# First batch element: x on ScalarE's queue, matrix pieces first on the two others; the last rows ahead of layer four's weights

## The chip, the cores and the metric

The kernel runs on one core of a Trainium2 chip. The core has five engines that run side by side, each with its own stream of instructions: TensorE (PE), VectorE (DVE), ScalarE (ACT), GpSimd (POOL) and SyncE (SP). They wait for each other through semaphores only. Transfers between device memory and the core's SBUF are issued by an engine into its own DMA queue. Three queues are used here: that of SP, that of ACT and that of POOL. All three feed the same 16 DMA engines. The metric is the device time of one execution in microseconds (us).

## What is computed

x is 16 elements of 1024 nodes by 128 features, adj 16 matrices of 1024 x 1024. All is float32.

```
# first block, per element
degree = adj.sum(-1)
gathered = einsum('bid,bij->bjd', x, adj) / degree
x = layernorm(x + relu(concat(x, gathered) @ W.T + b))
# second block: four layers; layers 3 and 4 also get the outputs of earlier layers as input
src = nodes @ ws + bs;  dst = nodes @ wd + bd;  own = nodes @ wn + bn
upd = concat(rownorm(adj) @ src, own, colnorm(adj).T @ dst)
nodes = tanh(upd @ wu + bu)
x = layernorm(x + nodes_of_layer_4)
```

rownorm and colnorm divide the rows and the columns of adj by their Euclidean norms.

## The kernel before

The elements are worked through one after the other. One matrix of 4 MB stays in SBUF while its element is computed, and the next one is loaded into a second buffer meanwhile. The order of the instructions on every engine is written out by hand: the Python program issues them in the order in which each engine executes them. `hooks` in a layer is a dictionary from the number of a matmul step to a function, which issues work on all engines just before that step.

Only the first element has nothing ahead of it to hide its loads. Its beginning is a program of its own.

- **Loads.** The matrix `a` of element one is cut into eight blocks of 128 rows, `k` of each half `h`. `load_pair(q, i, groups)` loads two blocks (a pair, 1 MB) with one DMA of 256 KB (a piece) for each group of 32 partitions. Groups 0 and 1 are issued by SP, 2 and 3 by POOL, for each of four pairs; the first two pairs are the second half. `load_nodes(q, h)` loads half an x, four DMAs of 64 KB, whose runs are 512 bytes long; the matrix has runs of 4096 bytes. `w0n` is the weight of the first block, 128 KB; `b0r` is its bias, read for all partitions.
- **First block.** TensorE runs three idle matmuls of zeros (`idle`, six passes, since a float32 matmul has two records), then transposes the second half of x (`xtr`, `to_xT(1)`), then `w0n` (`w0tr`). ACT copies both out of PSUM. Then follow the products of x and weights (`px`, four blocks), and for each pair the products `pa` of x and matrix as it arrives. ACT squares the blocks (`square`), DVE sums their rows (`degree`), POOL adds the squares. `pg` are the products of gathered nodes and weights; DVE turns them into x1n, with statistics, and `written` scales them. For block 0 of the second half `written` is an ACT instruction (L541), for the others one of DVE. `x1tr` transposes them.
- **Weights.** Each layer's weights are folded: `fetch_weights` loads ws, wd, wn and wu, `fold_begin` transposes the first three (`wtr`) and multiplies the biases (`bm`), `fold_end` multiplies by wu (`wm`) and saves the result to device memory (`wsave`). PSUM results called `small` share two banks, so a third one waits until ACT has copied out the first.
- **Transposed matrix.** The source side needs the matrix transposed. `load_rows(0, q, ...)` loads quarter q of the rows in another order (eight DMAs of 128 KB), `scale_rows` multiplies them on ACT by the inverse norms of the rows (eight instructions), `transpose_rows` transposes them on DVE. Quarters 2 and 3 make `at[1]`, 0 and 1 make `at[0]`.
- **Layer one** (`plain_layer`) has 34 matmul steps of two passes: 2 with the own weights, 16 with the matrix (half 1, half 0), 8 with `at[1]` and 8 with `at[0]`, from step 26. `last_loads` issues the loads of layer four's weights and of row quarter 1 on SP.

The DMAs of SP wait for one another through eight counters, which ACT's DMAs share: the ninth is issued when the first has landed. POOL has eight of its own.

Of the kernel before, what the change touches and what calls it, by code (L numbers as in the profile page):

```python
# [23 lines left out]
def adj_resnorm_kernel(ctx: ExitStack, tc: tile.TileContext, x, adj, w0, b0, layers, out):  # L24
# [33 lines left out]
    nc = tc.nc  # L58
    B, N, D = x.shape
    NB = N // P  # L60
# [8 lines left out]
    NJ = NB // 2  # L69
# [41 lines left out]
    ident = one.tile([P, HW], F32, tag="e0", name="ident")[:, :P]  # L111

    def own_weights(wm, l, c):

        if l == 3:
            at = dict(zip(PAIRED[l], (0, P))).get(c, 2 * P + SUMS)
            return wx[l][:, at:at + P]
        if l == 2:
            at = MREST + P * PAIRED[l].index(c)
            return wm[:, at:at + P]  # L120
        return wm[:, CHUNKS[l] + 1, :P]

    def message_weights_of(wm, l, c):

        if l in PAIRED:
            at = 2 * P * (1 + PAIRED[l].index(c)) if c in PAIRED[l] else MREST
            return by_parts(wm[:, at:at + 2 * P])
        return wm[:, 1 + c].rearrange("p (a v c) -> p a v c", a=2, v=2)
# [67 lines left out]
    def fetch_weights(raw, l, q, bc, wm=None):  # L196
        ws, bs, wd, bd, wn, bn, wu, bu = layers[l]
        nch = CHUNKS[l]
        size = max(3 * nch * P, KEPT[l] * 2 * P, WIDTH[l])
        flat = raw.take(size) if wm is None else wm[:, WIDTH[l]:]  # L200
        wr = flat[:, :3 * nch * P].rearrange("p (k c v) -> p k c v", k=3, c=nch)
        for k, w in enumerate((ws, wd, wn)):
            q.dma_start(wr[:, k], w.rearrange("(c p) v -> p c v", p=P))
        wur = raw.take(3 * P).rearrange("p (k v) -> p k v", k=3)
        q.dma_start(wur, wu.rearrange("(c p) v -> p c v", p=P))
        if wm is not None:
            wm = as_chunks(wm, l)
        else:
            wm = as_chunks(flat[:, :WIDTH[l]] if l in PAIRED else flat, l)
        return wr, wur, bc, wm, [raw.take(3 * P).rearrange("p (k v) -> p k v", k=3) for _ in range(nch)]  # L210

    def fold_begin(l, fetched, copy=nc.scalar.copy, later=False):

        wr, wur, bc, wm, wTs = fetched
        for c in range(CHUNKS[l]):
            name = f"wtr{l}_{c}"
            pt = small(name, [BPH, P]) if c < 2 else product(name).rearrange("p (k v) -> p k v", v=P)
            for k in range(3):
                nc.tensor.transpose(pt[:, k], wr[:, k, c], ident)
            copy(wTs[c], pt[:, :3])  # L220
        pm = small(f"bm{l}", [HW]) if CHUNKS[l] == 1 else product(f"bm{l}")
        for k in range(2):
            nc.tensor.matmul(pm[:, k * P:(k + 1) * P], bc[:, k:k + 1].to_broadcast([P, P]),
                             wur[:, PART[k]], start=True, stop=True)
        nc.tensor.matmul(pm[:, 2 * P:2 * P + 1], wur[:, PART[2]], bc[:, 2:3], start=True, stop=True)

        def biases():
            if l in PAIRED:
                nc.scalar.copy(by_parts(wm[:, :2 * P]), pm[:, :2 * P].rearrange("p (a v c) -> p a v c", a=2, v=2))
            else:  # L230
                nc.scalar.copy(wm[:, 0], pm[:, :2 * P])
            nc.scalar.activation(bout[l], pm[:, 2 * P:2 * P + 1], AF.Identity, bias=bc[:, 3:4])

        return biases if later else biases()

    def fold_end(l, fetched, chunks=None):
        _, wur, _, wm, wTs = fetched
        for c in range(CHUNKS[l]) if chunks is None else chunks:
            pm = small(f"wm{l}_{c}", [HW]) if c < 2 else product(f"wm{l}_{c}")
            for k in range(3):  # L240
                nc.tensor.matmul(pm[:, k * P:(k + 1) * P], wTs[c][:, k], wur[:, PART[k]],
                                 start=True, stop=True)
            nc.scalar.copy(message_weights_of(wm, l, c), pm[:, :2 * P].rearrange("p (a v c) -> p a v c", a=2, v=2))
            nc.scalar.copy(own_weights(wm, l, c), pm[:, 2 * P:3 * P])
        if l not in PAIRED:
            nc.sync.dma_start(wsave[l], wm.rearrange("p c v -> p (c v)")[:, :WIDTH[l]])
        elif l == 3:
            nc.sync.dma_start(wsave[l], wm)
# [6 lines left out]
    def small(name, shape=(K,)):  # L255
        return ps_s.tile([P, *shape], F32, tag="small", name=name)
# [11 lines left out]
    def product(name, i=None):  # L268
        if i is None:
            return ps_t.tile([P, HW], F32, tag="pt", name=name)  # L270
        return ps_p.tile([P, HW], F32, tag=f"p{i}", name=name)
# [135 lines left out]
    def root_inverses(cols, inv, s):  # L407
        nc.vector.tensor_scalar_max(cols[:, s], cols[:, s], NORM_EPS * NORM_EPS)  # L408
        nc.gpsimd.tensor_tensor(inv[:, s], cols[:, s], mhalf[:, s], ALU.pow)  # L409
# [271 lines left out]
    def load_rows(b, q, st):  # L681


        n = QB // len(st)
        for i, piece in enumerate(st):
            load_rows_piece(b, q, piece, i * n, n)
        return st

    def load_rows_piece(b, q, piece, k, n, groups=range(G)):
        v = adj[b, q * QB * C:(q + 1) * QB * C].rearrange("(k r) (h g j) -> h g r k j", r=C, h=NH, g=G)  # L690
        for g in groups:
            for h in range(NH):
                nc.sync.dma_start(piece[g * C:(g + 1) * C, :, h * P:(h + 1) * P], v[h, g, :, k:k + n])  # L693
        return piece

    def scale_rows(st, q, rinv, which=range(QB)):
        n = QB // len(st)
        for k in which:
            row = st[k // n][:, k % n]
            nc.scalar.activation(row, row, AF.Copy, scale=rinv[:, q * QB + k:q * QB + k + 1])  # L700
# [444 lines left out]
    w0n = one.tile([P, 2 * P], F32, tag="xb", name="w0n")  # L1145
# [4 lines left out]
    def load_pair(q, i, groups):  # L1150
        h, k = PAIRS[i]
        for g in groups:
            q.dma_start(a[g * C:(g + 1) * C, h * BPH + k:h * BPH + k + 2], av[h][g, :, k:k + 2])

    def load_nodes(q, h):
        for g in range(G):
            q.dma_start(xn[g * C:(g + 1) * C, h * BPH:(h + 1) * BPH], xv[h][g])

    idle = one.tile([P, HW], F32, tag="S2", name="idle")
    nc.vector.memset(idle, 0.0)  # L1160
    make_identity(nc, ident)
    load_nodes(nc.sync, 1)
    nc.gpsimd.dma_start(w0n, w0)
    for i in range(4):
        load_pair(nc.sync, i, (0, 1))
        load_pair(nc.gpsimd, i, (2, 3))
        if i == 1:
            load_nodes(nc.gpsimd, 0)
    biases_of = [[b0, *layers[0][1::2], *layers[1][1::2]], layers[2][1::2], layers[3][1::2]]
# [37 lines left out]
    places = {q: Q[i].rearrange("p k (u c) -> p (k u) c", u=2) for q, i in ((2, 2), (3, 3), (0, 4))}  # L1207
    places[1] = one.tile([P, 2 * NJ, HW // 2], F32, tag="T2", name="rows1_0")
    rows, fetched = {}, []
# [8 lines left out]
    def last_loads():  # L1218
        places_left = Places([one.tile([P, NJ, HW], F32, tag="T4", name="raw4").rearrange("p k i -> p (k i)"),
                              one.tile([P, N], F32, tag="x", name="raw4_x"),  # L1220
                              one.tile([P, HW], F32, tag="S4", name="raw4_s")])
        columns.append(places_left.take(len(biases_of[2])))
        fetched.append(fetch_weights(places_left, 3, nc.sync, columns[2]))
        rows[1] = load_rows(0, 1, [places[1]])

    nc.vector.memset(mhalf, -0.5)
    nc.vector.reduce_sum(fold[:, :C], ident.rearrange("p (g c) -> p c g", g=G), axis=AX.X)
# [94 lines left out]
    def written(h, q, write=norm_write):  # L1322
        mv, _, rstd, shift = of_half[h][1]
        v = x1n[:, h * BPH + q]
        write(v, v, (mv, rstd, shift), q)
# [47 lines left out]
    two_stats(1, 2)  # L1373
    root_inverses(cols, inv, slice(NB))
    biases()
    written(1, 0, norm_write_act)
    fold_end(0, fetched[0])
    biases = fold_begin(1, fetched[1], later=True)
    for q in range(1, BPH):
        written(1, q)  # L1380
# [26 lines left out]
    for b in range(B):  # L1407
# [8 lines left out]
        if b == 0:  # L1416
# [23 lines left out]
            def columns0(rows, h, engine=nc.vector):  # L1440
                scale_columns(a, cinv[0], rows, half(h), engine)
# [20 lines left out]
            def fold_last(destination, finish):  # L1462
                bias_columns(2)
                fold_begin(3, fetched[3])

            def first0(destination, finish):
                destination(0, cinv[0])
                columns0(range(NJ), 0)
                scale_rows(rows[1], 1, rinv)
                transpose_rows(rows[1], 1, at)  # L1470
                fold_last(destination, finish)

            def sums0(destination, finish):
                combine_1(y)
# [7 lines left out]
                for i in range(2):  # L1482
# [2 lines left out]
            hooks = {3: lambda *_: inverses(0, st0, NB), 5: weights0, 6: rows0,  # L1485
                     7: lambda *_: scale_rows(rows[0], 0, rinv), 8: cinv0,
                     9: lambda *_: transpose_rows(rows[0], 0, at), 10: second0,
                     14: lambda *_: columns0(range(NJ, NB), 0), 18: first0, 21: lambda *_: fold_end(3, fetched[3]),
                     26: sums0}
            T = {i: one.tile([P, NJ, HW], F32, tag=f"T{i}", name=f"T{i}_0") for i in (2, 3)}  # L1490
            plain_layer(b, 0, feats, t, wm, a, at, f1, "acc", hooks)
# [196 lines left out]
        if nxt:  # L1688
# [4 lines left out]
            rows = {}  # L1693
# [182 lines left out]
```

## Time and profile before

| | us |
|---|---|
| median of 3 runs | 2378.34 |
| lowest and highest | 2377.73, 2379.17 |
| the profiled execution's own time | 2378.45 |
| its span in the trace | 2376.6 |
| TensorE busy in the span | 2364.0 |
| TensorE busy, 0 to 62 us of the span | 55.90 |
| TensorE busy, 62 to 2360 us | 2298.00 |
| TensorE busy, 2360 to 2376.6 us | 10.13 |

The clock granted to TensorE was 0.999 over the span. All times of instructions below are counted from the beginning of the span. In a row of the timeline the first number is the start, the second the time until the group ended, and the brackets hold how long the engine had been idle before it and what released it. In a row of waits the numbers are the total, how often, and the longest. A name such as `wtr<-ident,raw` says what is written and what is read; L and a number is the line. A row of a DMA queue has packets, MB and the time of its packets as a share of 16 engines.

### The profile page before, as it was taken

The numbers are of one execution on the slowest core, as the hardware profiler recorded it, in microseconds if no ns is written. First come the engines' busy times: TensorE is split into PE (matmuls) and PEld (weight loads), VectorE is DVE, ScalarE is ACT, GpSimd is POOL, SyncE is SP. The second block draws the span as 40 slices with busy tenths as digits, with TensorE's granted clock in tenths as the row PEclk, the third lists the DMA queues.
The fourth block names the chain that finished last, engine by engine and source line by source line (L and its number), as shares of the span: only waits on it lengthen the run. The fifth ranks groups of instructions, "written<-read, shape, count | busy, mean of one in ns | idle before, by whom it ended". The sixth has DMA issues, their size and how long they took to land.

```text
span 2376.6 us, 39287 instructions
## 1 busy us (share of the span) xinstructions
PE 2364.0 (99%) x15268; PEld 1148.7 (48%) x15268; DVE 2094.5 (88%) x2830; ACT 980.9 (41%) x1858; POOL 278.5 (12%) x119
## 2 busy tenths in 40 slices
PE   9999999999999999999999999999999999999998
PEld 5455565555655555443534444344443444434444
DVE  7999998998988989889988889898899998998954
ACT  5425335352443524445243452534425334352322
POOL 5000111101111011111011110111100111101100
PEclk9999999999999999999999999999999999999999
DMA  9536263362734527244273442725336263362400
GB/s 226 110 89 144 58 138 76 80 139 49 158 62 98 116 54 166 52 105 106 63 157 70 100 94 72 152 65 121 82 77 145 58 140 75 80 139 49 101 22 22
DMA packets 363909, 232.10 MB, mean 98 GB/s; under 512 B 150758, under 2 KB 334827, under 8 KB 363723
## 3 DMA queue, kind: packets, MB, share of 16 engines
q1 hardware_dynamic: 360698, 226.24, 42.9%
q0 software_dynamic: 1200, 2.50, 0.4%
q8 instruction: 121, 1.98, 0.4%
q10 hardware_dynamic: 1824, 0.85, 0.1%
q14 instruction: 66, 0.53, 0.1%
HBM read 209.66 MB, written 19.84 MB: 97 GB/s over the span
## 4 chain that ended last, share of the span: by engine, by line
PE 97%; DMA 2%; SPq 0%; DVE 0%; ACT 0%; issue 0%; POOLq 0%; POOL 0%; ACTq 0%; DVEq 0%
PE m L1106 45%; PE z L1106 24%; PE pt L261 9%; PE pt_z L261 5%; PE m_f L636 5%; PE m3s L1106 2%; PE z_f L636 2%; PE pw L261 2%; DMA Q<-in_adj_dram 1%; DMA b0r<-in_L_gnn_b_dram 1%; PE pt_p L261 1%; PE z L925 1%; DMA raw<-in_L_gnn_wu_dram 0%; DMA a<-in_adj_dram 0%; DMA rows<-in_adj_dram 0%; SPq L693 0%
## 5 line engine op out<-in xcount | busy, mean ns | idle before, releaser
L1106 PE MATMUL m<-a,t 128*64 128x512 f32 x1008 | 425.1, 593 | 0.0
L1106 PE MATMUL m<-at,t 128*64 128x512 f32 x1008 | 420.4, 592 | 0.0
L1106 PE MATMUL m<-T,S 128*64 128x512 f32 (+1 forms) x1040 | 398.5, 572 | 0.0
L1106 PE MATMUL m<-Q,S 128*64 128x512 f32 x880 | 392.3, 592 | 0.0
L496 POOL TENSOR_TENSOR rs<-ve,mhalf 128x32 f32<-128x32 f32 x30 | 191.6, 6386 | 1019.2 <-DVE ve L494 1019.2
L1106 PE MATMUL z<-at,t 128*64 128x512 f32 (+1 forms) x520 | 229.6, 579 | 0.0
L1106 PE MATMUL z<-a,S 128*64 128x512 f32 x504 | 228.3, 592 | 0.0
L1106 PE MATMUL z<-Q,t 128*64 128x512 f32 (+1 forms) x520 | 227.5, 580 | 0.0
L1106 PE MATMUL z<-a,t 128*64 128x512 f32 (+1 forms) x520 | 227.4, 580 | 0.0
L1106 PE MATMUL z<-at,S 128*64 128x512 f32 x504 | 226.6, 592 | 0.0
L1106 PEld LDWEIGHTS m<-Q,S 128*64 128x64 f32 x880 | 119.4, 137 | 214.9 <-issue 213.2
L1106 PEld LDWEIGHTS m<-T,S 128*64 128x64 f32 x1040 | 128.8, 137 | 141.0 <-issue 135.9
L1106 PEld LDWEIGHTS m<-at,t 128*64 128x64 f32 x1008 | 131.4, 137 | 131.5 <-issue 131.5
L1106 PEld LDWEIGHTS m<-a,t 128*64 128x64 f32 x1008 | 129.7, 137 | 114.0 <-issue 107.0
L958 ACT COPY e<-m 64x512 f32<-64x512 f32 x63 | 36.7, 582 | 340.2 <-PE m L1106 339.8
L1106 PE MATMUL z<-T,t 128*64 128x512 f32 (+2 forms) x400 | 173.0, 575 | 0.0
L409 POOL TENSOR_TENSOR inv<-cols,mhalf 128x16 f32<-128x16 f32 (+1 forms) x16 | 50.0, 3126 | 933.9 <-DVE cols L408 933.9
L448 DVE TENSOR_TENSOR a<-a,cinv 128x512 f32<-128x512 f32 x256 | 155.5, 682 | 0.0
L336 ACT ACTIVATE sq<-a 128x1024 f32<-128x1024 f32 x120 | 125.9, 1050 | 37.5 <-DVE acc L343 23.4
L1106 PEld LDWEIGHTS z<-Q,t 128*64 128x64 f32 x520 | 69.6, 137 | 122.6 <-issue 121.9
L331 ACT ACTIVATE a<-a 128x1024 f32<-128x1024 f32 x120 | 125.4, 1045 | 0.4
L261 PE MATMUL pt<-wm,f1T 128*64 128x128 f32 (+1 forms) x1536 | 120.5, 308 | 0.0
(338 smaller groups left out, 4925.5 us busy)
## 6 DMA issues: line engine op xcount, KB each, us to landing
a<-in_adj_dram SPq DMA_DIRECT2D x120, 512.0 KB, 12.8
rows<-in_adj_dram SPq DMA_DIRECT2D x480, 64.0 KB, 2.2
a<-in_adj_dram SPq DMA_DIRECT2D x240, 128.0 KB, 3.4
wm<-wsave SPq DMA_DIRECT2D x32, 704.0 KB, 4.4
wm<-wsave SPq DMA_DIRECT2D x31, 320.0 KB, 3.0
xs<-in_x_dram SPq DMA_DIRECT2D x60, 128.0 KB, 3.4
cinv<-dr SPq DMA_DIRECT2D x30, 256.0 KB, 6.6
dinv<-dr SPq DMA_DIRECT2D x30, 256.0 KB, 6.6
```

Source lines behind the costliest of these rows:

```text
L261: nc.tensor.matmul(out[s], x[:, s], y, start=start, stop=stop)
L331: nc.scalar.activation(a[:, i, :], a[:, i, :], AF.Copy, accum_out=degree)
L336: nc.scalar.activation(sq, a[:, i, :], AF.Square, accum_out=state["cols"][:, i:i + 1])
L409: nc.gpsimd.tensor_tensor(inv[:, s], cols[:, s], mhalf[:, s], ALU.pow)
L448: engine.tensor_mul(a[:, i, s], a[:, i, s], cinv[:, s])
L496: nc.gpsimd.tensor_tensor(rstd, ve, mhalf[:, :n], ALU.pow)
L636: nc.tensor.matmul(o, x_, y_, start=start, stop=stop)
L925: nc.tensor.matmul(nodes(o) if len(y.shape) == 4 else o, x_, y, start=start, stop=stop)
L958: nc.scalar.copy(e0[high], A[high])
L1106: nc.tensor.matmul(o, x, y_, start=start, stop=stop)
```

## The change

Three things are changed, all of them in the program of element one. The instructions stay the same; only their order on the engines and the queue of four DMAs change.

1. The second half of x is issued by ACT, as its first four instructions, no longer by SP ahead of the matrix. SP begins with its eight matrix pieces. POOL begins with its two pieces of the first pair; the building of the identity matrix (`make_identity`, POOL) and the load of `w0n` follow behind them, ahead of the second pair.
2. `fold_end(0)`, with two ACT copies, is issued ahead of `written(1, 0, norm_write_act)`, with one ACT instruction.
3. In `last_loads` the row quarter 1 is loaded ahead of layer four's weights. Its scaling on ACT is issued at step 11 of layer one, no longer at 18, where it stood ahead of the bias columns and the folding of layer four. These are issued at step 19, and `fold_end(3)` at 22 instead of 21. The transposition of quarter 1 on DVE stays at 18.

```diff
-    make_identity(nc, ident)
-    load_nodes(nc.sync, 1)
-    nc.gpsimd.dma_start(w0n, w0)
+    load_nodes(nc.scalar, 1)
     for i in range(4):
         load_pair(nc.sync, i, (0, 1))
         load_pair(nc.gpsimd, i, (2, 3))
+        if i == 0:
+            make_identity(nc, ident)
+            nc.gpsimd.dma_start(w0n, w0)
         if i == 1:
             load_nodes(nc.gpsimd, 0)
...
+        rows[1] = load_rows(0, 1, [places[1]])
         columns.append(places_left.take(len(biases_of[2])))
         fetched.append(fetch_weights(places_left, 3, nc.sync, columns[2]))
-        rows[1] = load_rows(0, 1, [places[1]])
...
+    fold_end(0, fetched[0])
     written(1, 0, norm_write_act)
-    fold_end(0, fetched[0])
     biases = fold_begin(1, fetched[1], later=True)
...
             def first0(destination, finish):
                 destination(0, cinv[0])
                 columns0(range(NJ), 0)
-                scale_rows(rows[1], 1, rinv)
                 transpose_rows(rows[1], 1, at)
-                fold_last(destination, finish)
...
+                     11: lambda *_: scale_rows(rows[1], 1, rinv),
-                     14: lambda *_: columns0(range(NJ, NB), 0), 18: first0, 21: lambda *_: fold_end(3, fetched[3]),
+                     14: lambda *_: columns0(range(NJ, NB), 0), 18: first0, 19: fold_last,
+                     22: lambda *_: fold_end(3, fetched[3]),
                      26: sums0}
```

## The prediction

> **What bounds the kernel now.** I read the page's busy times first, then who TensorE waited for before and after 62 us, then its timeline in the first 34 us, and last the packets of each DMA queue in short stretches.
>
> ```profile
> PE 2364.0 (99%) x15268; PEld 1148.7 (48%) x15268; DVE 2094.5 (88%) x2830; ACT 980.9 (41%) x1858; POOL 278.5 (12%) x119
> ```
>
> TensorE is busy for 2364.0 of 2376.6 us. Whatever shortens this kernel takes idle time from TensorE, and only 12.6 us are there. Its waits from 0 to 62 us, and then from 62 us to the end:
>
> ```profile
> PE pa L1258 <- DMA a<-in_adj_dram: 1.3, 2, 1.0
> PE wtr L219 <- ACT raw L1185: 1.3, 1, 1.3
> PE bm L223 <- ACT wm L244: 1.3, 1, 1.3
> PE px L1286 <- ACT w0T L1204: 0.7, 1, 0.7
> ...
> PE on L1793 <- DVE f23T L1788: 0.4, 1, 0.4
> ```
>
> The diff can reach three of them: two waits for the matrix (0.33 and 1.01 us), one at `wtr` and one at `bm` (1.28 each). With `px` that is 4.6 us, 0.19%, the most that could be gained. The timeline (start, duration, instruction, idle time before) shows where they sit:
>
> ```profile
> 6.74 0.80 PE L1194 MATMUL xtr<-ident,xn 128*128 128x128 f32 x4
> ...
> 9.97 3.67 PE L1258 MATMUL pa<-a,xn 128*128 128x512 f32 x8 [0.33 <-DMA a<-in_adj_dram]
> 14.65 1.95 PE L1258 MATMUL pa<-a,xn 128*128 128x512 f32 x4 [1.01 <-DMA a<-in_adj_dram]
> ...
> 32.02 0.71 PE L223 MATMUL bm<-raw 128*128 128x128 f32 x4 [1.28 <-ACT wm L244]
> ...
> 32.71 0.63 PE L1330 MATMUL x1tr<-ident,x1n 128*128 128x128 f32 x4
> ```
>
> The first useful work is `xtr`, the transpose of x's second half. It comes before everything else in TensorE's order, and it needs all four x pieces. They were alone on the SP queue and had landed by 4.8 us (issue at 2.1, 2.7 us to landing). The rows that decide are the packets of the queues (packets, MB, share) in 2.5 to 3, 3 to 3.5, 19 to 20 and 22 to 22.5 us, where q1 is SP's and q0 POOL's:
>
> ```profile
> q1 hardware_dynamic: 188, 0.09, 57.6%
> ...
> q0 software_dynamic: 32, 0.11, 75.8%
> q1 hardware_dynamic: 58, 0.02, 17.9%
> ...
> q0 software_dynamic: 66, 0.21, 78.7%
> q1 hardware_dynamic: 67, 0.07, 28.3%
> ...
> q1 hardware_dynamic: 144, 0.07, 44.9%
> ```
>
> Two busy queues move equal numbers of packets, not equal bytes. From 17 to 18 us both carry 4 KB packets: 50 of POOL's to 49, 0.17 MB to 0.16. At 19 us SP carries mostly 512-byte packets (b0 and first weights): still 67 to 66, but 0.07 MB to 0.21. Alone, SP then does 144 such packets in half a microsecond; beside POOL's large ones it did 67 in a whole one. At 3 us x's own packets fell from 188 to 58 per half microsecond, just while w0's 128 KB passed.
>
> **Part 1: x on ACT's queue, matrix first.** x's second half is 512 packets of 512 bytes, 32 per DMA engine, with four completion packets 36. Before, they ran in front of the matrix in SP's queue. Now SP (from 0.74 instead of 2.59 us) and POOL (0.74 instead of 2.21) put 4 KB packets beside them from the start, and each x packet waits for one of each. When x has had its 36 turns, SP has had 36 too, four data and one completion per piece: 7.2 pieces of 256 KB, 1.9 MB. POOL the same, with w0 and small packets among them, some 1.8. With x that is 3.9 MB. By the windows, before had moved 0.55 MB at 5 us and 3.9 at 17.2. The queues fill now at about 2.5 us instead of the lull of 96 to 131 GB/s up to 5 us, worth some 0.4 MB at 0.27 MB/us: 1.5 us. So the last turn comes near 15.7 us, and the slowest DMA engine some 0.5 later (SP's pieces landed while the mean was most of a piece ahead): x lands at 16.2 us. Bounds: 5.5 if queues shared by bytes (256 KB at a third of 0.27 MB/us from 1.8 us, 4.7, and landing), 18.5 if x ended with the whole matrix. I take 16.2, because the 19 us row is the nearest: small packets of a hardware queue beside large ones. At the best rate seen, 0.33 MB/us from 1.8 us on, it is 13.6.
>
> SP can't run dry and free x earlier: SP's and ACT's DMAs share eight completion counters, so SP's pieces 5, 7 and 8 wait for x's pieces 1, 2 and 3, but piece 7 is issued at x's 18th turn while SP holds work to its 30th.
>
> The Trainium skill, "DMA: Bandwidth & Descriptors", section "Queues, rings and completion order", says that each engine round-robins between queue rows by packets; the 67 to 66 agrees. Its section "Issuing engines are not separate DMA queues" says that a second issuing engine only saves issue time; by that rule alone this part would gain at most SP's 1.85 us of issue.
>
> Then TensorE: from `xtr` at 6.74 to `wtr` at 27.69 are 20.95 us, less the waits for the matrix, now long landed, 19.6. `wtr` starts at 16.2 + 19.6 = 35.8, so 8.1 us late. ACT and DVE keep pace: ACT's squares (8 of 1.14 us and two copies) end 14 us after `xtr`; the copy behind them is needed after 17.
>
> Moved steps that cost nothing: ACT's four issues (0.42 each) stand before its table load (1.28), over at 3.9, first needed at 7.58. POOL's identity ends near 2.4 instead of 1.31; DVE idles until 9.96. w0 stands behind two matrix pieces: POOL's first 640 KB landed near 9.05, start 0.7 earlier now and meet more of SP's, so 8.6 instead of 4.6. x hides it; without that cover `w0tr` is 1.2 late.
>
> Clock: TensorE stands still from 6.95 to 16.2. No row shows what follows so long a stop. Bounds: nothing (after the 1.01 us stop passes follow at 0.43 us), and 2.6 us, what the six warm-up passes from rest lost at 0.855 us each (weight loads at 3.33, 4.18, 5.03) against 0.43. A 9 us stop is nearer to rest; ACT's copies (0.73) hide some: 2.0. The skill, "TensorE: Matmul & The Clock Gate", Part 1, has half clock after about 3.4 us idle and as long to come back; by that 1.7, and the total 0.3 lower.
>
> **Part 2: folding one ahead of `written(1, 0)` on ACT.** The 1.28 before `bm` goes: ACT copied `wm` only at 31.45, 1.0 after TensorE had written it, because L541 in front waited for POOL. But `x1tr` needs DVE's last `written`, which ends at 32.55; it started at 32.71. Gain 0.15; the rest turns into a wait of `x1tr`. Behind the moved L541 wait only copies needed later.
>
> **Part 3: rows 1 before layer four's weights.** ACT scaled rows 1 from 57.16, when the last landed, to 60.46, and the bias copy that frees `wtr`'s bank stood behind it. Eight row DMAs now pass four weight DMAs of 768 KB, 3.0 us at 0.26 MB/us: landed near 54, scaled by 57.5 at hook 11, when ACT would idle (51.8 to 57.2). The weights land near 57.2 instead, needed after 59.0, one step later than before, and with part 1 later still. Gain 1.28, less 0.1 for a bank. Weight folding at 22 delays the save of the weights by under 1 us; SP's x loads behind it are needed at 120.9.
>
> **Sum.** 8.1 + 2.0 - 0.15 - 1.2 = 8.75, on 2378.45 us of the profiled execution (span 2376.6, 0.1 above the median of 2378.34): 2387.2. TensorE is busy without a wait from 62 us, so nothing later gives it back. I forecast 2387.
>
> **Rivals.** (1) ACT's queue isn't held to turns, x lands by 6.5 us. For it: POOL's x (64 KB pieces beside SP's matrix) landed 0.6 us apart, more bytes than equal turns of 512 bytes give; but at 13 to 15 us POOL's packets there averaged 2 KB, so it isn't a like case. Then w0 decides: 8.6, 0.9 for transpose and copy, 1.15 for `px`, so `pa` at 10.65, and after its 3.67 the second pair at 14.3 instead of 14.65 (landed near 13.2): 0.35, and with 0.15 and 1.2 a gain of 1.7: 2376.7, not slower. The point is x at 9.4 us (9.4 - 8.1 - 1.35 = 0). (2) Part turns: the completion of x comes between 8 and 13.5 us because engines overlap packets. At 10.5: 2.4 late at `wtr`, about 1 for the clock, less 1.35: 2380.5, within 0.2%. (3) Turns hold, but the stop leaves the clock up and 0.33 MB/us is reached: 13.6 instead of 16.2: 2382.6.
>
> **Chances.** Forecast 0.72 (2383.1 to 2390), (1) 0.13, (2) 0.09, (3) 0.06. 0.2% (4.8 us) is about what a measurement tells from no change: slower 0.72 and a little of (2) and (3), 0.75; same 0.22; faster 0.03, since 4.6 us is all there is. Range 2380.5 to 2390: x at 18.5 with the full clock price gives 2390, and below 2380.5 stand (1) and half of (2). The forecast's own range is 2383 to 2390.
>
> **What would show it.** x's four issues on ACT with 10 to 15 us to landing, `xtr` starting near 16 after a wait of some 9 us, weight loads at 0.85 us spacing after it, no wait for the matrix, `wtr` without its 1.28, `x1tr` waiting for DVE. I am wrong if x lands by 8 us; then the first wait is `w0tr`'s for w0.

## The result, and the profile after

The changed kernel takes 2383.70 us (median of 16 runs, 2382.29 to 2385.08), the kernel before beside it 2378.66 (16 runs, 2377.62 to 2382.19). The ratio is 1.0019 with a 95% interval of 1.0011 to 1.0027: 5.0 us slower, inside the range, 3.3 us below the predicted 2387.0. The profiled execution took 2382.46 us with a span of 2380.6, so it is 4.0 us longer than the profiled execution of before.

The row of busy times on the changed kernel's page:

```profile
PE 2365.6 (99%) x15268; PEld 1361.2 (57%) x15268; DVE 2094.2 (88%) x2830; ACT 980.1 (41%) x1858; POOL 278.6 (12%) x119
```

TensorE has the same instructions as before; its idle time grew from 12.6 to 15.0 us, and its busy time by 1.6. Its waits, from 0 to 62 us and from there to the end (total, how often, longest):

```profile
PE xtr L1195 <- DMA a<-in_adj_dram: 6.8, 1, 6.8
...
PE px L1287 <- ACT w0T L1205: 0.5, 1, 0.5
PE bm L223 <- ACT wm L244: 0.3, 1, 0.3
PE wm L241 <- DVE rinv L424: 0.2, 1, 0.2
...
PE on L1794 <- DVE f23T L1789: 0.3, 1, 0.3
```

The three waits that the diff could reach are gone or short: none for the matrix, none at the `wtr` of step 18, 0.30 left at `bm`. One new wait of 6.85 us takes their place. It is written down to the matrix, because a matrix piece landed at about the same moment, but `xtr` doesn't read the matrix. What it needs is x: x's fourth piece was issued at 2.14 us and took 10.8 us to land, and SP's next DMA, which waits for that piece's counter, goes out at 12.94 us:

```profile
12.94 0.35 SPq L1211 DMA_DIRECT2D b0r<-in_L_gnn_b_dram  x1
```

TensorE's timeline (start, duration, instruction, and in brackets the idle time before and its releaser):

```profile
13.06 1.09 PE L1195 MATMUL xtr<-ident,xn 128*128 128x128 f32 x4 [6.85 <-DMA a<-in_adj_dram]
...
16.96 6.33 PE L1259 MATMUL pa<-a,xn 128*128 128x512 f32 x12
...
34.37 0.49 PE L219 MATMUL wtr<-ident,wm 128*128 128x128 f32 x3
...
38.41 0.94 PE L1331 MATMUL x1tr<-ident,x1n 128*128 128x128 f32 x4
...
46.08 1.95 PE L261 MATMUL pt<-wm,x_T 128*64 128x256 f32 x16
...
65.78 0.22 PE L1185 MATMUL biases<-ident,biases 4*128 4x4 f32 x1
65.93 1.20 PE L219 MATMUL wtr<-ident,raw 128*128 128x128 f32 x9
...
67.56 2.82 PE L925 MATMUL z<-at,t 128*128 128x512 f32 x6
```

The same stretch of before, in rows that the prediction doesn't show:

```profile
27.69 0.49 PE L219 MATMUL wtr<-ident,wm 128*128 128x128 f32 x3
...
39.74 1.95 PE L261 MATMUL pt<-wm,x_T 128*64 128x256 f32 x16
...
60.56 0.88 PE L219 MATMUL wtr<-ident,raw 128*128 128x128 f32 x6 [1.28 <-ACT raw L1185]
...
61.86 2.82 PE L925 MATMUL z<-at,t 128*128 128x512 f32 x6
```

Side by side, the two give the account of the 4.0 us between the profiled executions. `xtr` starts at 13.06 instead of 6.74: 6.32 late. From `xtr` to the first `wtr` before needed 20.95 us, 1.34 of them waits for the matrix, so 19.61 of work; now it needs 21.31. The 1.70 more is the clock: after the stop the first long passes `pa` load their weights 0.85 apart, and from 19.26 on 0.43 apart. The rows of the weight loads (PEld):

```profile
17.82 0.34 PEld L1259 LDWEIGHTS pa<-a,xn 128*128 128x128 f32 x1 [0.52 <-issue]
18.67 0.34 PEld L1259 LDWEIGHTS pa<-a,xn 128*128 128x128 f32 x1 [0.52 <-issue]
19.26 0.19 PEld L1259 LDWEIGHTS pa<-a,xn 128*128 128x128 f32 x1 [0.26 <-issue]
19.69 0.19 PEld L1259 LDWEIGHTS pa<-a,xn 128*128 128x128 f32 x1 [0.24 <-issue]
```

This is what half speed means below. So `wtr` is 6.68 late. From there to the last sixteen products `pt` (46.08 instead of 39.74) 0.34 comes back, and at step 18, where `biases` and all nine `wtr` now follow each other without a gap, 1.50: the fourth pass of the products `z` of that half starts at 68.07 instead of 63.23, 4.84 late. That lateness stays: the last long group of TensorE starts at 2354.06 instead of 2349.41, 4.65 late. From its end the profiled execution needed 21.8 us more, that of before 22.5, which makes the 4.0 of the spans. That 0.7 lies behind TensorE's work, at the storing of the result; the median of the times is 5.0 longer.

### The profile page after: what moved, and what is told of

It reads as the page before. It is cut to its first block, busy times and chain, and to the rows that moved or that the text cites. A ratio compares the mean times of both kernels' runs of the same rounds, so it can differ in the third digit from the quotient of the medians.

```text
span 2380.6 us, 39290 instructions
## 1 busy us (share of the span) xinstructions
PE 2365.6 (99%) x15268; PEld 1361.2 (57%) x15268; DVE 2094.2 (88%) x2830; ACT 980.1 (41%) x1858; POOL 278.6 (12%) x119
## 4 chain that ended last, share of the span: by engine, by line
PE 98%; DVE 1%; DMA 1%; POOL 0%; ACT 0%; issue 0%; POOLq 0%; DVEq 0%
PE m L1106 43%; PE z L1106 26%; PE pt L261 9%; PE pt_z L261 5%; PE m_f L636 5%; PE z_f L636 3%; PE pw L261 2%; PE m3s L1106 2%; PE z L925 1%; PE pt_p L261 1%; PE d L925 1%; PE pa L1259 1%; DMA a<-in_adj_dram 0%; DMA xn<-in_x_dram 0%; PE px L1287 0%; PE wm L241 0%
## 5 line engine op out<-in xcount | busy, mean ns | idle before, releaser
L1106 PEld LDWEIGHTS m<-T,S 128*64 128x64 f32 x1040 | 134.3, 137 | 118.7 <-issue 113.7
L261 PEld LDWEIGHTS pt<-wm,f1T 128*64 128x64 f32 x1536 | 114.3, 137 | 23.6 <-issue 13.5
```

What stands on the lines that cost most here:

```text
L261: nc.tensor.matmul(out[s], x[:, s], y, start=start, stop=stop)
L1106: nc.tensor.matmul(o, x, y_, start=start, stop=stop)
```

## The experiments

Each kernel was timed against the kernel before on the same chip; that one stood at 2378.49, 2378.45 and 2378.74 us in the three sessions.

### Part 1 alone

```diff
-    make_identity(nc, ident)
-    load_nodes(nc.sync, 1)
-    nc.gpsimd.dma_start(w0n, w0)
+    load_nodes(nc.scalar, 1)
     for i in range(4):
         load_pair(nc.sync, i, (0, 1))
         load_pair(nc.gpsimd, i, (2, 3))
+        if i == 0:
+            make_identity(nc, ident)
+            nc.gpsimd.dma_start(w0n, w0)
```

> The kernel before with part 1 alone (x on ACT's queue, matrix first). My theory: part 1 brings the whole loss, and by making TensorE 6 to 7 us late it also hides the wait at `wtr` that part 3 was to remove, since the rows have long landed. So x lands near 13 us, `wtr` of layer one starts near 34.4 us, the 1.28 us before `bm` stay, those before `wtr` at step 18 are gone, and the time is 2383.5 to 2384.5, as after or up to 0.5 more. Rival: the parts add up, so that part 3's 1.3 us have to be taken off the kernel after to get here: 2385 to 2386.

Measured: 2382.65 us (2381.95 to 2383.88, 11 runs), ratio 1.0018 with 1.0009 to 1.0026. The time is under both expected ranges, while the steps are those of the theory: `xtr` starts at 13.21, after a wait of 7.22, and `wtr` at 34.23. The timeline of TensorE at step 18 holds the surprise:

```profile
64.86 0.22 PE L1185 MATMUL biases<-ident,biases 4*128 4x4 f32 x1
65.01 1.20 PE L219 MATMUL wtr<-ident,raw 128*128 128x128 f32 x9
```

Part 1 alone makes the whole loss, as near as the runs can tell: 4.2 us by the medians, and in the traces the last long group of TensorE starts at 2354.18, beside 2354.06 in the changed kernel. And without part 3 the 1.28 us gap ahead of the last six `wtr` is gone too: with TensorE 6.3 us late, rows 1 land and are scaled in time. So in the changed kernel part 3 has nothing left to gain.

### Parts 2 and 3 alone

The other two parts of the diff, with the loads in their old order.

> The kernel before with parts 2 and 3 alone; the first loads as before. My theory: 0.3 us from the folding moved ahead on ACT and 1.3 to 1.5 us from the wait at step 18, so 2376.7 to 2377.1, x landed by 5 us. Rival one: DVE, busy without a gap from 53 to 76 us, takes the place of the wait, and the time is that of before, 2378.5. Rival two: the weights of layer four, now loaded last, are late at step 19: no gain or a loss, and a wait of `wtr` or `bm` for a DMA.

Measured: 2375.95 us (2375.34 to 2378.61, 11 runs), ratio 0.9988 with 0.9979 to 0.9997. They gain 2.5 us, more than forecast. The profiled execution was 1.5 over the median; its timeline has another stop, at the first product with the matrix:

```profile
11.17 7.08 PE L1258 MATMUL pa<-a,xn 128*128 128x512 f32 x12 [2.68 <-DMA a<-in_adj_dram]
```

The twelve passes take 7.08 us here, where before needed 3.67 for eight and 1.95 for four: half speed for a while, behind a late piece of the matrix. If the parts added up, the change would cost 4.2 - 2.5 = 1.7 us. It costs 5.0, since the loss of part 1 covers the gap that part 3 removes.

### Part 3 alone, and its loads alone

Part 3 alone (loads, scaling at 11, folding at 19):

> Part 3 alone (rows of quarter 1 loaded ahead of layer four's weights, their folding behind the scaling). Theory (the gain of parts 2 and 3 together, 2.5 us, is nearly all part 3's, since x1tr takes back what bm gives): the gaps at step 18 go, bm keeps its 1.28 before it, x1tr takes 0.63; 2376.2 to 2377.2. Rival (the two parts add as gaps removed, 1.28 each): 2377.2 for this one, with 1.0 to 1.3 for part 2, and not under 2377.0.

Measured: 2375.92 us (2375.15 to 2376.43, 11 runs), ratio 0.9989 with 0.9980 to 0.9998. That is under the expected range; all of the gain of parts 2 and 3 is part 3's. Next, of part 3 the order of the loads alone, scaling and folding left at 18:

```diff
+        rows[1] = load_rows(0, 1, [places[1]])
         columns.append(places_left.take(len(biases_of[2])))
         fetched.append(fetch_weights(places_left, 3, nc.sync, columns[2]))
-        rows[1] = load_rows(0, 1, [places[1]])
```

> Of part 3 the order of the loads alone: quarter 1's eight row DMAs ahead of layer four's weights, scaling and folding at step 18 as before. Theory (the loads are the cause; ACT has nothing between cinv, over at 51.8, and this scaling, so the hook it is issued at doesn't matter): the scaling runs from 54.9 to 58.2, the bias copy follows the biases at once, the 1.28 before the second wtr goes, and the whole gain of part 3 is there: 2375.7 to 2376.4. Rival (the folding must also go a step later, since at 58.6 the weights, now landing near 57.2, or the banks are not ready): a gap of 0.5 to 1.3 us stays at the wtr of step 18 and the time is 2377.0 to 2378.2.

Measured: 2376.19 us (2375.70 to 2377.66, 11 runs), ratio 0.9988 with 0.9979 to 0.9997. ACT's timeline and TensorE's at step 18 of this kernel:

```profile
54.85 3.31 ACT L700 ACTIVATE rows<-rows,rinv 128x256 f32<-128x256 f32 x8 [3.62 <-DMA raw<-in_L_gnn_wn_dram]
58.77 0.16 ACT L1185 COPY raw<-biases 128x4 f32<-128x4 f32 x1 [0.61 <-PE biases L1184]
...
58.52 0.22 PE L1184 MATMUL biases<-ident,biases 4*128 4x4 f32 x1
58.67 1.20 PE L219 MATMUL wtr<-ident,raw 128*128 128x128 f32 x9
```

The scaling begins at 54.85 instead of 57.16 and is over at 58.16, before `biases`, so the copy that frees the bank follows at once. The other moved lines make no difference that the times can tell (2376.19 and 2375.92): ACT has nothing between `cinv` and this scaling, so the step it is issued from doesn't matter. The eight DMAs in front of the weights are the gain.

### Part 2 alone

```diff
-    written(1, 0, norm_write_act)
     fold_end(0, fetched[0])
+    written(1, 0, norm_write_act)
```

> Part 2 alone: the wm copy on ACT ahead of written(1, 0). Theory (x1tr takes it back): the gap before bm goes from 1.28 to 0.30, x1tr lasts 0.94 instead of 0.63 and wm waits 0.16; from wtr at step 27.7 to the 16 products pt 11.7 to 11.9 us instead of 12.05; 2378.1 to 2378.5, no difference that can be measured. Rival (a gap removed is a gain): 2377.2 to 2377.5.

Measured: 2378.50 us (2377.72 to 2382.24, 11 runs) beside 2378.74, ratio 0.9998 with 0.9989 to 1.0007: nothing that can be measured. The row shows where the 1.28 went. TensorE's timeline of this kernel:

```profile
30.51 0.71 PE L223 MATMUL bm<-raw 128*128 128x128 f32 x4 [0.30 <-ACT wm L244]
...
31.20 0.42 PE L1330 MATMUL x1tr<-ident,x1n 128*128 128x128 f32 x2
31.79 0.59 PE L1330 MATMUL x1tr<-ident,x1n 128*128 128x128 f32 x2 [0.17 <-DVE x1n L537]
...
38.24 0.94 PE L241 MATMUL wm<-raw 128*128 128x128 f32 x6 [0.16 <-DVE rinv L424]
39.11 1.95 PE L261 MATMUL pt<-wm,x_T 128*64 128x256 f32 x16
```

`bm` comes 0.98 earlier, `x1tr` starts its first two blocks and then waits for DVE's, and `wm` waits for DVE once more. From the first `wtr` (27.15) to `pt` 11.96 us pass, in before 12.05: 0.09 is left.

The profiled execution of this kernel happened to be its longest, 2382.24, and it explains more than part 2. Its timeline at step 18:

```profile
58.10 0.55 PE L219 MATMUL wtr<-ident,raw 128*128 128x128 f32 x3
61.27 1.54 PE L219 MATMUL wtr<-ident,raw 128*128 128x128 f32 x6 [2.63 <-ACT raw L1185]
62.61 1.06 PE L223 MATMUL bm<-raw 128*128 128x128 f32 x4
...
63.75 4.72 PE L925 MATMUL z<-at,t 128*128 128x512 f32 x6
```

The rows came later here (scaling from 57.88), TensorE stood for 2.63 us instead of 1.28, and then ran at half speed: six `wtr` in 1.54 instead of 0.88, six `z` in 4.72 instead of 2.82. From that `wtr` to the first product behind the folding 9.05 us pass (61.27 to 70.32), in the profiled before 5.97 (60.56 to 66.53): 3.08 lost to the clock, by a stop only 1.35 longer. Such stops could be a part of why part 3 gains 2.5 us while its trace shows only 1.50 at step 18 (0.14 early ahead of it, 1.64 behind it). But the profiled executions of part 3 alone and of the kernel before are 2.5 us apart as well, and neither has such a stop: TensorE's last long group starts 1.83 earlier (2347.58 and 2349.41), and from its end to the end of the span 21.8 us pass instead of 22.5. Of 97 runs of the kernel before, 16 were above 2380 us, 1.6 to 4.6 over the medians; of the 22 runs of the two kernels with only the rows in front, one was 1.5 over its median and the others less than 0.6. That those 16 had this stop is argued from one trace, not shown, and the 2.68 us stop at the matrix, in parts 2 and 3 alone, is a rival for them.

### The two halves of part 1

x on ACT's queue, SP straight to the matrix, and POOL's order as before:

```diff
     make_identity(nc, ident)
-    load_nodes(nc.sync, 1)
+    load_nodes(nc.scalar, 1)
     nc.gpsimd.dma_start(w0n, w0)
```

> The kernel before, with x's second half on ACT's queue and SP beginning with the matrix; POOL still builds the identity first, then loads w0, then its first pair. Theory (SP's matrix packets beside x make nearly all the loss; x got 1.5 to 1.8 turns for each of SP's packets): x lands at 11.5 to 13, only a little earlier than the 13.06 of the whole change, since POOL's pieces join 1.5 us later; 2381.5 to 2383. Rival (POOL's earlier pieces are an equal part of the cause): x lands at 8.5 to 10, and the time is 2378.5 to 2380.

Measured: 2382.11 us (2380.91 to 2383.33, 11 runs), ratio 1.0013 with 1.0004 to 1.0022; `xtr` starts at 12.05. The queue of x alone costs 3.7 us, nearly the 4.2 of both halves. The other half, x on SP in front as before, POOL's first pair ahead of the identity and `w0n`:

```diff
-    make_identity(nc, ident)
     load_nodes(nc.sync, 1)
-    nc.gpsimd.dma_start(w0n, w0)
     for i in range(4):
         load_pair(nc.sync, i, (0, 1))
         load_pair(nc.gpsimd, i, (2, 3))
+        if i == 0:
+            make_identity(nc, ident)
+            nc.gpsimd.dma_start(w0n, w0)
```

> The kernel before, with x on SP's queue in front as before, and only POOL's order changed: its first pair ahead of the identity and w0. Theory: x's packets take turns with POOL's large ones from about 2.5 us; before, 188 had gone per half microsecond alone and 58 beside w0, so the remaining 390 of 576 take 3.4 us at 58 per half microsecond (5.8 at the 67 per microsecond of 19 to 20 us): x lands at 6.5 to 9, w0 at 8 to 9, xtr begins 0 to 2.2 late and w0tr waits for w0. 2378.8 to 2380.8. Rival (the matrix on SP alone makes the loss; POOL's order costs nothing since the first pair comes earlier): 2378.0 to 2378.6.

Measured: 2380.13 us (2379.24 to 2381.18, 11 runs), ratio 1.0008 with 0.9999 to 1.0016. The time fell into the expected range by other steps than those expected. TensorE's timeline:

```profile
6.87 0.63 PE L1195 MATMUL xtr<-ident,xn 128*128 128x128 f32 x4
11.25 0.69 PE L1204 MATMUL w0tr<-ident,w0n 128*128 128x128 f32 x2 [3.75 <-DMA w0n<-in_L_gnn_W_dram]
12.40 2.07 PE L1287 MATMUL px<-w0T,x_T 128*128 128x128 f32 x8 [0.46 <-ACT w0T L1205]
```

x wasn't late at all, but w0 landed at 11.25 (issued at 3.15, 8.1 to landing) and TensorE stood for 3.75 us; the `px` behind it ran at half speed. The packets of the queues from 3 to 4 and from 4 to 5 us (packets, MB, share; q1 carries x here, q0 is POOL's) show that the turns I had expected weren't taken throughout:

```profile
q0 software_dynamic: 36, 0.14, 45.6%
q1 hardware_dynamic: 38, 0.02, 6.6%
...
q1 hardware_dynamic: 241, 0.11, 60.0%
q0 software_dynamic: 47, 0.13, 59.5%
```

In the first microsecond they went about one for one, in the next five small packets of SP's for one of POOL's. The halves cost 3.7 and 1.7 us (the second's interval reaches down to no change) and together 4.2: while TensorE waits for x, w0's lateness costs nothing.

### Smaller packets of the matrix

The changed kernel with every matrix piece cut into two DMAs of 2 KB runs, so that each of SP's and POOL's turns moves half the bytes. It was timed once.

```diff
         for g in groups:
-            q.dma_start(a[g * C:(g + 1) * C, h * BPH + k:h * BPH + k + 2], av[h][g, :, k:k + 2])
+            for s in (0, 1):
+                q.dma_start(a[g * C:(g + 1) * C, h * BPH + k:h * BPH + k + 2, half(s)],
+                            av[h][g, :, k:k + 2, half(s)])
```

> The kernel after with every matrix piece of element one loaded as two DMAs over half of the columns, so that its runs are 2048 bytes long instead of 4096; the same bytes in twice as many packets. If x waits for packets (each of its 512-byte packets for one or so of every other queue), what passes between two of its packets is half as long, and x lands near 8 us instead of 13, and the first transposition with it. Rival: x's packets are slow for themselves under load, or the queues share in proportion to bytes: x lands at 12 to 13 us all the same.

Measured: 2383.1 us. TensorE's waits up to 62 us:

```profile
PE biases L1187 <- issue: 2.7, 1, 2.7
PE w0tr L1206 <- DMA w0n<-in_L_gnn_W_dram: 2.5, 1, 2.5
...
PE xtr L1197 <- DMA xn<-in_x_dram: 1.1, 1, 1.1
```

x landed at 7.3 us, nearly six earlier, with no change to x: the packet size of the other queues is what holds it. The edit also halves the bytes that the counters let a queue have on its way, but neither queue had run empty: up to 6 us SP had moved 0.52 MB of eight DMAs of 128 KB issued, POOL 0.32 of seven. So the mechanism of part 1 stands. As in the run above, w0 then decides (`w0tr` at 10.38). The 2.7 us ahead of `biases` at 32.5 appeared with this edit and took the rest of the gain; perhaps because POOL has twice as many matrix DMAs to issue. That link was not tested.

### More warm-up

The changed kernel with nine idle matmuls of zeros instead of three, so that TensorE doesn't stand still while x is on its way.

```diff
-    for _ in range(3):
+    for _ in range(9):
         nc.tensor.matmul(pt, idle[:, :P], idle, start=True, stop=True)
```

> The kernel after with nine idle matmuls instead of three ahead of the first transposition (they compute zeros that nobody reads). They keep TensorE busy until about 11.5 us, while x lands near 13. Theory of the clock: the passes after the wait run at 0.43 us from the start instead of 0.85, `wtr` comes 1.7 us earlier counted from `xtr`, and the time falls by 1.5 to 1.7 us against the kernel after, to about 2382. Rival: the passes after the wait are slow because the matrix is still arriving or ACT is late; then nothing changes, 2383.7.

Measured: 2381.37 us (2380.13 to 2384.65, 11 runs), ratio 1.0012 with 1.0003 to 1.0021. Over the kernel before that is 2.9 us, where the changed kernel has 5.0 and part 1 alone, in the same session, 4.2: 1.3 to 2.2 us less, beside a clock price of 1.7. The intervals reach some 2 us either way, so the size isn't settled; the sign is as the clock theory has it. Its profiled execution was one of the three longest (2383.96). There x landed at 13.86, the stop was 2.89 us, and `px` still took 2.07 us instead of 1.16: half speed again. From `xtr` to `wtr` it needed 21.99 us, 0.68 more than the changed kernel, so this trace doesn't show a clock price saved; why the median is lower stays open.

### x in front on two queues

Parts 2 and 3 kept; x's four pieces ahead of every matrix piece, two issued by SP and two by ACT, so that they go out in half the time.

```diff
-    make_identity(nc, ident)
-    load_nodes(nc.sync, 1)
+    for g in range(G):
+        (nc.sync, nc.scalar)[g % 2].dma_start(xn[g * C:(g + 1) * C, BPH:2 * BPH], xv[1][g])
     nc.gpsimd.dma_start(w0n, w0)
...
+        if i == 0:
+            make_identity(nc, ident)
```

> Parts 2 and 3 kept; x's four pieces still ahead of every matrix piece, but two issued by SP and two by ACT, w0 first on POOL, then its first pair, and the identity behind it. Theory (x is late only where large packets stand beside it; if all small ones go first, a second issuing engine costs nothing): SP's matrix begins 0.85 us earlier, POOL's 0.6; x lands at 4.8 to 6.0 and xtr begins by 6.8, the waits for the matrix (0.33 and 1.01) go in part; 2375.0 to 2376.2, that is at most 1 us below parts 2 and 3 alone (2375.95). Rival (the earlier matrix packets catch the end of x): x lands at 7 to 8.5 and the time is 2376.5 to 2377.5.

Measured: 2377.55 us (2376.62 to 2379.19, 11 runs), ratio 0.9996 with 0.9987 to 1.0005. The time is the rival's, the step is neither's. TensorE's timeline:

```profile
6.36 0.60 PE L1196 MATMUL xtr<-ident,xn 128*128 128x128 f32 x4
...
11.59 7.08 PE L1260 MATMUL pa<-a,xn 128*128 128x512 f32 x12 [2.52 <-issue]
```

x was not late; `xtr` follows the idle matmuls without a wait. But the first product with the matrix came only at 11.59, although SP began the first pair 0.9 us earlier; in the traces with the old order of loads it came at 9.80, 9.86, 9.97, 10.33 and 11.17. From 4 to 5 us SP moved 80 packets and POOL 14, and the pair needs the pieces of both. That POOL lost what SP gained fits this, but one window of one trace doesn't show it. And the twelve `pa` took 7.08 us, with weight loads 0.85 apart from 13.1 to 15.7: a stop of 2.52 us was enough for half speed, as the 2.68 us stop was in parts 2 and 3 alone.

No kernel here beats part 3 alone, 2375.92; and each other start of the first element tried here has a longer median than the old one with the same other parts.

## Why the prediction was right, and which terms were off

The place, the direction and the wait were right: x beside large packets, `xtr` first, nothing that gives it back. The time lies only 0.7 us inside the forecast's own range of 2383 to 2390, and that is in part luck: x landed at 12.94 us, in the span that rival (2) had claimed (8 to 13.5), its four pieces took 5.3 to 10.8 us to land where the forecast's sign was 10 to 15, and two errors behind the 16.2 partly cancel, as the first point below shows.

- **"Each x packet waits for one of each", x landed at 16.2 us.** The kind of mechanism is right: 2 KB packets on the other queues brought x to 7.3. One for one it was not. The size is off by 3.1 us, the largest miss of the sum. The row I took for it, 67 packets to 66 at 19 us, was not a law of equal turns. The packets of the changed kernel from 4 to 5, 5 to 6 and 7 to 8 us (q10 is ACT's queue with x, q1 SP's, q0 POOL's):

```profile
q1 hardware_dynamic: 43, 0.13, 70.6%
q10 hardware_dynamic: 68, 0.03, 21.5%
...
q0 software_dynamic: 28, 0.11, 46.7%
q1 hardware_dynamic: 22, 0.07, 38.2%
q10 hardware_dynamic: 82, 0.04, 23.5%
...
q1 hardware_dynamic: 59, 0.19, 75.3%
q0 software_dynamic: 23, 0.05, 19.7%
q10 hardware_dynamic: 86, 0.04, 17.3%
```

  Here x got 1.5 to 3.7 packets for one of SP's; in the other microseconds from 2 to 11 it was 0.9 to 3.6. Up to 12 us it moved 575 of its 576, SP 379 and POOL 252. So only 2.63 MB, not 3.9, had gone by 12.94 us. That was at a lower rate than the 0.27 MB/us of the working, 0.24 from 4 to 12 us (1.89 MB); the two errors partly cancel.
- **"`wtr` starts at 16.2 + 19.6 = 35.8", 8.1 late.** The sum of work held: `wtr` starts at 34.37, 21.31 behind `xtr`, that is 19.61 and the clock. The lateness is 6.68 with the clock, where the prediction had 10.1.
- **Clock, 2.0.** 1.70, as what is left of the 21.31; the weight loads 0.85 us apart show its cause. Measured the same way, the two other traces with x on ACT and `xtr` late gave 1.41 and 1.55, so 2.0 was too high. The estimate from the Trainium skill's "TensorE: Matmul & The Clock Gate", Part 1, was 1.7, the nearer of the two. Its idle window of about 3.4 us isn't a safe limit here, though: stops of 2.45, 2.52, 2.63, 2.68, 2.70 and 2.89 us were all followed by half speed, while stops of up to 1.28 us between two pieces of work were not. The traces have none in between. The page also calls the window free-running, and a position that differs from execution to execution would fit that.
- **Part 2, 0.15.** The wait moved to `x1tr`, as forecast. The whole part is worth 0.09 in its own trace and nothing in the times. In the changed kernel 0.34 came back on this stretch, which one trace cannot tell from that.
- **Part 3, 1.2.** 1.50 came back at step 18. But the attribution failed: part 1 alone closes that gap as well. The prediction added the two as if they were independent. In its sum this did no harm, because the gap is gone once, whoever removes it; as a statement of what part 3 brings to this kernel it was wrong. On the old start part 3 is worth 2.5.
- **"TensorE is busy without a wait from 62 us, so nothing later gives it back."** Right: 4.84 late at 68 us and 4.65 at 2354.
- **"w0 stands behind two matrix pieces … 8.6"; "x hides it".** It was hidden, but w0 landed at 12.2 us (issued at 3.13, 9.1 to landing), 0.7 before x. So rival (1) was priced wrongly: with x early, `w0tr` had to wait until 11.25 in the run with POOL's order alone, and not until 8.6. Its 2376.7 would have been nearer 2380.13 - 2.5 = 2377.6, an estimate from the runs on POOL's order and on part 3.

With the measured sizes the sum is 6.32 + 1.70 - 1.34 - 0.34 - 1.50 = 4.84, against the 8.75 of the prediction; 3.1 of the difference is the landing of x.

The page named in the prediction, the Trainium skill's "DMA: Bandwidth & Descriptors", says under "Queues, rings and completion order" that engines take turns by packets, and gives such a packet as some 9 to 17 descriptors. That need not be the packet that the profile counts, of which x has one for each run of 512 bytes. The run with 2 KB packets agrees that packet size decides; the counts 68 to 43 and 241 to 47 don't agree with equal turns of the profile's packets.

## What to carry to other kernels

A small load that everything waits for belongs in front of the large ones, on a queue that nothing else has filled yet. On a second queue it shares turns with 4 KB packets: x's last piece of 64 KB, in 512-byte packets, then took 10.8 us instead of 2.7. Ask of every gap that a change removes whether another part of the same change, by being late, has already removed it. And where TensorE stands still for some 2.5 us or more, count half speed on top: in one trace the 1.35 us longer wait at step 18 cost 3.08 more in the passes behind it.

## What the runs showed that I had not expected

- Shares between queues are far from even, in either direction. By the microsecond, small packets of SP's or ACT's got 0.9 to 5 turns for one large packet of another queue.
- An earlier start of SP's half of the matrix, by 0.9 us, didn't bring the first product with it any sooner: 11.59, beside 9.80 to 11.17 with the old order.
- A wait can be written down to the wrong load. `xtr`, which reads only x, was shown as waiting for the matrix for 6.85 us.
- The place of eight DMAs in SP's order decided 2.5 us by the medians, twice the gap that the trace showed at step 18; 1.50 of it is seen there. With part 3 alone the scatter of the times was smaller too, 2375.15 to 2376.43 over 11 runs, where the kernel before had 2377.07 to 2381.31 over 33; with parts 2 and 3, which have the same loads there, it was 2375.34 to 2378.61.
